# A graph layer's edge groups: one at a time, or in pairs

## The chip, the cores and the metric

The kernel runs on 1 core of a Trainium2 chip. The metric is the device time of one execution in microseconds (us); lower is better. The engines are PE (TensorE, the matrix engine; its weight loads are shown as PEld), DVE (VectorE), ACT (ScalarE), POOL (GpSimd) and SP (SyncE). SP, ACT and POOL also issue DMAs, each from its own queue. Every engine runs its own instruction stream in order and waits for others through semaphores.

## The reference, cut to what matters

N = 12,500 nodes with 64 features, E = 200,000 edges sorted by `dst`, all in float32.

```python
def ssp(x): return softplus(x) - log(2.0)
nodes    = x[[src, dst]]                                # (E, 128): both ends of each edge
gates    = ssp(edge_attr @ We1 + be1) @ We2 + be2       # (E, 64)
gates    = gates * (1 - sigmoid(5 * (dist - 3.5)))      # "cut" below
h        = ssp(nodes @ Wn1 + bn1) @ Wn2 + bn2           # (E, 64)
sums     = zeros(N, 64).at[dst].add(h * gates)          # the messages, added up per node
new      = x + ssp(sums @ Ws1 + bs1) @ Ws2 + bs2
out      = layernorm(x + new)
```

## The kernel before

The edges go in 391 groups of 512 (`NG` = 391). A group has two halves of 256 edges (h = 0, 1) and each half two blocks of 128 (t = 0, 1), so four blocks (k). As `dst` is sorted, the destinations of a half lie in a window of `W` = 42 consecutive nodes; `sums` stays in SBUF, with features on the partitions and nodes along the row (half 0 on partitions 0 to 63, half 1 on 64 to 127).

The code lies under a manual schedule: each engine's instructions stand in the order in which the Python code emits them, and a framework adds the semaphore waits from the tiles that an instruction reads and writes. Each of the tile names below has a number of buffers that are used in turn, and a new use waits for the last reader of the old one.

A prologue (to about 146 us) computes `table` = x @ Wn1 (the lower half) + bn1 for all nodes and writes it to DRAM, computes `cut`, and starts gathers. Then comes the loop over steps i = -1 to 388. In step i, each with the functions and profile lines that matter:

- `load` (L278, L286, on SP): one DMA of 256 KB of edge features for two groups (`eT`), and for each group two DMAs that put the window's 42 table rows below the constant rows of `wns`. They wait for an old scatter.
- `fetch` (L257, on SP and ACT): rows of x for a few blocks come by single-row DMAs, 7 a step on SP and 9 a step on ACT, between ACT's other instructions in threes.
- `gather` (L231, on POOL): the other blocks' rows of x by indirect DMA, 128 rows each, up to four a group; `xg` has 19 buffers (`AHEAD` 14 + `BEHIND` 5). POOL has no other work in the loop, so it runs ahead until a buffer is missing: the gathers of group g wait for the scatter of group g - 19, the last reader of that buffer.
- `transposes` (L307, L304, PE): the four blocks of group i+1, rows of x beside the one-hot of the destination in the window, become features by edges in PSUM (`tx`). `xcopy` (L314, ACT) copies that to SBUF (`xT`).
- `layer1_bias` (L319), `layer1_edge` (L324), `layer1_node` (L330), all PE: the first layer of group i+1 into `z` (two PSUM banks): 256 columns for the edges, where the two halves share the partitions, and 512 for the nodes, where the one-hot rows pick the destination's term from `wns`. The node matmuls wait for `xcopy`.
- `exps` (L341) and `logs` (L344) on ACT and `softplus` (L349) on DVE: softplus of the 768 columns into `s`.
- `layer2_bias` (L354), `layer2_edge` (L361), `layer2_node` (L366), PE: the second layer of group i, edge-major: blocks of `s` are the stationary operand, so its result `gh` has edges on the partitions: 2 matmuls of 128 columns and 4 of 64, which the profile shows as 4 and 8 records (a float32 matmul has two).
- `hcut` (L375) and `message` (L379) on DVE: h times `cut`, times the gates, 256 columns each.
- `scatter` (L383, PE): the messages of an older group times the one-hots, 84 columns, into a free part of `z`; `window` (L400, DVE) adds that to `sums`, two adds of 42 columns. `behind_by(i)` says which group: two behind, and from `CLOSE` = 12 steps before the end on one behind.
- `onehot` (L293, DVE) of group i+3; parts of `node_block` (the update and layernorm of up to 512 finished nodes, 25 blocks) at steps planned by `BLOCK_STEPS`.

So PE's order in a step is transposes i+1, biases, scatter, layer 1 edges i+1, layer 1 nodes i+1, layer 2 i. ACT's is copy, exp, log with three fetches behind each. DVE's is window sums, h, message, softplus, one-hot. POOL's is the gathers alone.

PSUM has eight banks: `z` two tiles of two banks, `gh` and `tx` two of one each.

Of the kernel before, what the change touches and what calls it, by code (L numbers as in the profile page):

```python
# [42 lines left out]
F32 = mybir.dt.float32  # L43
# [14 lines left out]
P = 128  # L58
# [10 lines left out]
SPREADS = 5  # L69
PREPARE = 5  # L70
BEHIND = 5
CLOSE = 12


BLOCK_STEPS = ((2, 3, 4, 4, 6, 7, 8, 9, 10, 14), (2, 3, 3, 4, 5, 6, 7, 8, 9, 10), (1, 2, 1, 2, 3))
# [48 lines left out]
def gnn_resnorm_kernel(ctx: ExitStack, tc: tile.TileContext, a: dict, out: bass.AP, E: int):  # L124
# [53 lines left out]
    one = const.tile([P, 1], F32, name="one")  # L178
    half = const.tile([P, 1], F32, name="half")
    eps = const.tile([P, 1], F32, name="eps")  # L180
    ones3 = const.tile([PIECES, HE], BF16, name="ones3")
    be3 = const.tile([PIECES, 2, D], BF16, name="be3")
    row3 = const.tile([PIECES, 2, K, D], BF16, name="row3")
    rs3 = const.tile([PIECES, K, D], BF16, name="rs3")
    wns = const.tile([DW, REST, 2, 2 * D], F32, name="wns")

    xgs, xrs, eTs = {}, {}, {}
    made = {}

    def note(key, ins):  # L190
# [80 lines left out]
    bases = {}  # L271

    def load(g):
        old = ("scatter", g - LOADS - 4)
        if g % 2 == 0:
            n = min(2, NG - g)
            both = loads.tile([P, 2, HE], F32, name="eT", bufs=4)
            behind(note(("load", g), nc.sync.dma_start(both[:, :n], a["eT"][:, g : g + n, :])), old)  # L278
            for j in range(n):
                eTs[g + j] = both[:, j]  # L280
            _, at = nc.values_load_multi_w_load_instructions(
                base_i[32:33, 2 * g : 2 * g + 4], engines=[SP], min_val=0, max_val=8 * D * (N - 1),
                skip_runtime_bounds_check_because="they were clamped to these bounds")
            bases[g], bases[g + 1] = at[:2], at[2:]
        for h in range(2):
            behind(note(("load", g), nc.sync.dma_start(  # L286
                wns[D:DW, g % REST, h, :].bitcast(U8),
                table_bytes[:, bass.ds(bases[g][h], 8 * D * W)].rearrange("o (w f) -> (o w) f", w=W))), old)
# [27 lines left out]

    def layer1_bias(g, *needs):
        zs[g] = z_tile()
        first = nc.tensor.matmul(zs[g][:, 0, :HE], be3.rearrange("q h d -> q (h d)"), ones3, start=True, stop=False,  # L319
                                 skip_group_check=True)  # L320
        behind(first, *needs)

# [14 lines left out]

    def exps(g, part=every):
        if part.start == 0:
            us[g] = work.tile([P, 3 * HE], F32, name="u")  # L340
        nc.scalar.activation(us[g][:, part], z_of(g)[:, part], AF.Exp)  # L341

    def logs(g, part=every):
# [1 line left out]

    def softplus(g, part=every):
        if part.start == 0:
            ss[g] = work.tile([P, 3, 2, P], F32, name="s", bufs=3)
        nc.vector.scalar_tensor_tensor(ss[g].rearrange("p i t e -> p (i t e)")[:, part], us[g][:, part], BIG,  # L349
                                       z_of(g)[:, part], OP.min, OP.max)  # L350

# [43 lines left out]
    def window(g):  # L395
        if g not in window_at:
            window_bases(g)
        for h in range(2):
            part = sums[h * D : (h + 1) * D, bass.ds(window_at[g][h], W)]
            nc.vector.tensor_add(part, part, scs[g][h * D : (h + 1) * D, h * W : (h + 1) * W])  # L400

    def node_block(first, n, pool):

# [86 lines left out]
    with tc.manual_schedule():  # L490
# [4 lines left out]
        with tc.tile_pool(name="prep", bufs=1) as prep:  # L495
# [81 lines left out]
                    nc.vector.tensor_sub(rest, rest, pieces[:, q, :])  # L577
            nc.scalar.dma_start(row_d.rearrange("(o q) f -> o q f", o=1), pieces)
            rows = prep.tile([PIECES, 4, D], BF16, name="rows")
            nc.scalar.dma_start(rows.rearrange("q i d -> q (i d)"), row_d)  # L580
            for i in range(3, PARTS):
                load_x(i)
# [3 lines left out]
            for i in range(PARTS):  # L586
                for c in range(i * CP, (i + 1) * CP, CP // 2):
                    m = CP // 2
                    ps = z_tile().rearrange("p b (k f) -> p (b k) f", k=K)
                    for k in range(m):  # L590
                        nc.tensor.matmul(ps[:, k, :], xT[:, c + k, :], wnb, start=True, stop=True)  # L591
                    tb = prep.tile([P, m, 2 * D], F32, name="tb", bufs=6)
                    nc.scalar.copy(tb[:, :K, :], ps[:, :K, :])
                    nc.vector.tensor_copy(tb[:, K:, :], ps[:, K:m, :])
                    nc.sync.dma_start(by_node[:, c : c + m], tb)
                    nc.vector.memset(sums[:, c * P : WIDE if c + m == NCH else (c + m) * P], 0.0)
                if i == 1:
                    nc.vector.tensor_copy(base_i[:1], base_b[:1])
                    nc.vector.tensor_scalar(base_i[32:33], base_b[32:33], float(8 * D), None, OP.mult)
                    nc.vector.tensor_scalar(rows_i, rows_i, float(4 * D), None, OP.mult)  # L600
                    for k in range(2):
                        nc.vector.tensor_copy(be3[:, k, :], rows[:, 0, :])
                    for k in range(K):
                        nc.vector.tensor_copy(row3[:, :, k, :], rows[:, 1:3, :])
                        nc.vector.tensor_copy(rs3[:, k, :], rows[:, 3, :])
                if i == 2:
                    nc.scalar.activation(dist, dist, AF.Sigmoid, bias=steep, scale=-5.0)
                    nc.scalar.preload_act_table_set("natural_log_exp_and_others")
                    nc.vector.tensor_copy(rel, dst_i)
                    for t in range(2):  # L610
                        r = rel[:, :, 2 * t : 2 * t + 2]
                        nc.vector.tensor_sub(r, r, base_b[:, :NH].rearrange("p (g h) -> p g h", h=2))


        with tc.tile_pool(name="finish", bufs=1) as finish:
            blocks = list(zip(node_blocks(N), block_steps(N, NG)))
            last = NG - 1
            parts, begun, complete, rest = {}, None, 0, []

            def at(f, g, *more):  # L620
                if 0 <= g < NG:
                    f(g, *more)

            def behind_by(i):
                close = last - CLOSE
                return [g for g in ([i - 2] if i <= close else []) + ([i - 1] if i >= close else []) if g >= 0]

            for g in range(LOADS - 1):
                load(g)
            for g in range(2):  # L630
                onehot(g)
            for i in range(-1, last - 1):
                now = parts.pop(i, [])
                early = [part for part in now if part.tensor]
                at(load, i + LOADS)
                read_rows(i, 0, ROWS[0])
                fetch(i, 0, ROWS[0])
                if i >= 0:
                    at(gather, i + AHEAD)
                transposes(i + 1, ("load", i + 1), ("gather", i + 1), ("onehot", i + 1))  # L640
                xcopy(i + 1)
                read_rows(i, 1, ROWS[1])
                fetch(i, 1, ROWS[1] - 6)
                layer1_bias(i + 1)
                at(layer2_bias, i)
                for n, g in enumerate(behind_by(i)):
                    scatter(g, zs[i + 1][:, 1, HE + 2 * n * W : HE + 2 * (n + 1) * W])
                layer1_edge(i + 1)
                layer1_node(i + 1)
                exps(i + 1)  # L650
                fetch(i, 1, 3)
                logs(i + 1)
                fetch(i, 1, 3)
                for g in behind_by(i):
                    window(g)
                at(layer2, i)
                for part in early:
                    part.tensor(tx_tile())
                at(hcut, i)
                at(message, i)  # L660
                softplus(i + 1)
                for part in early:
                    part.others()
                at(onehot, i + 3)
                for part in now:
                    if not part.tensor:
                        part.others()
                complete = i
                if blocks and complete >= blocks[0][1] - PREPARE and not begun:
                    begun = node_block(*blocks[0][0], finish)  # L670
                    begun.pop(0).others()
                if blocks and complete >= blocks[0][1]:
                    steps = next(steps for steps in BLOCK_STEPS if i + steps[-1] < last - 1)
                    for n, part in zip(steps, begun):
                        parts.setdefault(i + n, []).append(part)
                    rest = begun[len(steps) :]
                    blocks.pop(0)
                    begun = None
            assert len(blocks) == 1 and begun and not parts


# [43 lines left out]
    with tc.If(far > 0), tc.tile_pool(name="outside", bufs=1) as o:  # L725
# [7 lines left out]
        with tc.For_i(0, NG, 1) as g:  # L733
# [20 lines left out]
            for k in range(K):  # L754
# [1 line left out]
            xT = o.tile([P, NB], F32, name="xT2")  # L756
            nc.vector.tensor_copy(xT, z[:, 0, :])
            z = z_tile()
            nc.tensor.matmul(z[:, 1, :HE], be3.rearrange("q h d -> q (h d)"), ones3, start=True, stop=False,
                             skip_group_check=True)  # L760
            nc.tensor.matmul(z[:, 1, :HE], we1.rearrange("a h d -> a (h d)"), e, start=False, stop=True,
                             skip_group_check=True)
# [110 lines left out]
```

## Time and profile before

| | |
|---|---|
| median of 10 runs | 2680.15 us (2665.99 to 2698.31) |
| the profiled execution's own time | 2677.73 us |
| its span, first to last instruction | 2675.9 us |
| mean granted TensorE clock | 0.825 |
| busy: PE, PEld, DVE | 2216.0, 1731.5, 1050.9 us |
| busy: ACT, POOL | 968.4, 1437.0 us |
| gathers (L231) | 1516, mean 948 ns, idle before them 1138.8 us |
| first and last copy (L314) of the loop | start at 146.4 and 2652.2 us |

A line of a timeline reads: start in us, duration in us, engine, source line, operation, output<-inputs, shape, count, and in brackets how long the engine had been idle and what ended that. A line of a group reads: line, engine, operation, tiles, count, then busy us and mean ns of one, then the idle time before and its releasers. Ends of matmuls are modelled; releasers are inferred, and "remote" or "issue" stand where none was found. PEclk is the clock that the throttle granted, as a share of full speed.

### The profile page before, as it was taken

How to read it: one execution, taken by the hardware profiler on the slowest of the kernel's cores; microseconds unless marked ns; L12 is line 12 of the kernel's file. 1: busy time of each engine (PE TensorE's matmuls, PEld its weight loads, DVE VectorE, ACT ScalarE, POOL GpSimd, SP SyncE). 2: the span in 40 equal slices, each digit the busy share in tenths (PEclk: the TensorE clock that was granted, in tenths of full speed). 3: DMA queues.
4: the chain of work that ended last, by engine and by line, in shares of the span. 5: the costliest groups of instructions: out<-in, count | busy, mean ns of one | idle time of the engine just before them, and what ended most of it. 6: DMA issues, size and time to landing. Idle time of an engine off the chain costs nothing.

```text
span 2675.9 us, 47845 instructions
## 1 busy us (share of the span) xinstructions
PE 2216.0 (83%) x11373; PEld 1731.5 (65%) x11373; DVE 1050.9 (39%) x2767; ACT 968.4 (36%) x1318; POOL 1437.0 (54%) x1520
## 2 busy tenths in 40 slices
PE   2388889888888888888888888889889888888897
PEld 1366667666666666666666666666667666666676
DVE  1233333333334343343333444434434444444445
ACT  0133333333333333333333433333333433333344
POOL 7335555555555555555555555555555555555530
PEclk9987877878888788788887878888877988778788
DMA  6222212212222222222222222222222222222210
GB/s 159 75 69 53 49 47 47 48 46 52 48 50 50 49 52 50 49 47 52 51 47 51 50 54 52 51 51 56 53 48 52 53 57 54 51 51 51 50 49 21
DMA packets 150911, 143.53 MB, mean 54 GB/s; under 512 B 51887, under 2 KB 98395, under 8 KB 150626
## 3 DMA queue, kind: packets, MB, share of 16 engines
q1 hardware_dynamic: 94090, 88.26, 11.7%
q0 software_dynamic: 48512, 49.77, 9.5%
q10 hardware_dynamic: 8024, 2.37, 0.4%
q8 instruction: 97, 1.59, 0.2%
q14 instruction: 188, 1.54, 0.2%
HBM read 130.59 MB, written 9.63 MB: 52 GB/s over the span
## 4 chain that ended last, share of the span: by engine, by line
PE 61%; ACTq 11%; another core or an unknown queue 11%; ACT 7%; issue 6%; DVE 2%; POOL 1%; DMA 1%; DVEq 0%; SPq 0%; POOLq 0%
PE z L330 15%; PE gh L366 11%; ACTq L257 10%; PE z L383 10%; PE gh L361 7%; PE tx L307 6%; ACT xT L314 6%; PE z L324 3%; PE gh L354 3%; PE z L319 2%; PE tx L419 1%; PE z L591 1%; POOL xg L231 1%; ACTq L245 1%
## 5 line engine op out<-in xcount | busy, mean ns | idle before, releaser
L231 POOL DMA_INDIRECT xg<-in_x,src_i x1516 | 1436.7, 948 | 1138.8 <-issue 355.0
L330 PE MATMUL z<-xT,wns 106*128 106x256 f32 x1564 | 564.3, 496 | 340.8 <-ACT xT L314 330.2
L330 PEld LDWEIGHTS z<-xT,wns 106*128 106x128 f32 x1564 | 355.8, 242 | 503.7 <-ACT xT L314 431.4
L341 ACT ACTIVATE u<-z 128x768 f32<-128x768 f32 x392 | 317.0, 809 | 809.1 <-PE z L330 352.5
L366 PE MATMUL gh<-consts,s 128*128 128x64 f32 x3128 | 488.1, 311 | 0.0
L366 PEld LDWEIGHTS gh<-consts,s 128*128 128x128 f32 x3128 | 483.3, 236 | 0.1
L400 DVE TENSOR_TENSOR sums<-sums,z 64x42 f32 x778 | 153.0, 197 | 838.1 <-issue 621.8
L314 ACT COPY xT<-tx 106x512 f32<-106x512 f32 x391 | 228.6, 585 | 681.1 <-remote 260.5
L375 DVE TENSOR_TENSOR h<-gh,cut 128x256 f32<-128x256 f32 x391 | 166.0, 425 | 634.2 <-PE z L383 271.2
L344 ACT ACTIVATE u<-u,one 128x768 f32<-128x768 f32 x392 | 365.9, 933 | 70.2 <-issue 55.8
L349 DVE SCALAR_TENSOR_TENSOR s<-u,z 128x768 f32<-128x768 f32 x392 | 369.2, 942 | 10.9 <-ACT u L344 9.8
L361 PEld LDWEIGHTS gh<-consts,s 128*128 128x128 f32 x1564 | 295.6, 240 | 69.1 <-DVE s L349 32.6
L383 PEld LDWEIGHTS z<-xg,msg 128*128 128x128 f32 x1556 | 237.6, 219 | 151.0 <-issue 146.7
L361 PE MATMUL gh<-consts,s 128*128 128x128 f32 x1564 | 305.2, 328 | 1.8 <-DVE s L349 1.8
L383 PE MATMUL z<-xg,msg 128*128 128x84 f32 x1556 | 303.0, 324 | 0.9 <-DVE msg L379 0.2
L324 PE MATMUL z<-eT,consts 128*128 128x256 f32 x782 | 291.9, 460 | 0.0
L307 PE MATMUL tx<-consts,xg 128*106 128x128 f32 x1517 | 276.9, 311 | 6.4 <-DMA wns<-table 6.4
L307 PEld LDWEIGHTS tx<-consts,xg 128*106 128x106 f32 x1517 | 215.1, 168 | 10.4 <-issue 7.7
L379 DVE TENSOR_TENSOR msg<-gh,h 128x256 f32<-128x256 f32 x391 | 165.9, 424 | 13.4
L354 PE MATMUL gh<-row,ones 3*128 3x512 bf16 x391 | 168.4, 431 | 0.0
L324 PEld LDWEIGHTS z<-eT,consts 128*128 128x128 f32 x782 | 140.0, 224 | 1.2 <-issue 1.2
L293 DVE TENSOR_TENSOR xg<-consts,rel 128x168 f32<-128x168 f32 x391 | 129.1, 330 | 0.0
(93 smaller groups left out, 612.7 us busy)
## 6 DMA issues: line engine op xcount, KB each, us to landing
xr<-in_x ACTq DMA_DIRECT2D x3328, 0.2 KB
eT<-in_eT SPq DMA_DIRECT2D x195, 256.0 KB
xr<-in_x SPq DMA_DIRECT2D x2688, 0.2 KB
xg<-in_x,src_i POOLq DMA_INDIRECT x1516
wns<-table SPq DMA_DIRECT2D x782, 21.0 KB
table<-tb SPq DMA_DIRECT2D x14, 448.0 KB
sums<-in_xT SPq DMA_DIRECT2D x7, 455.0 KB
y<-in_x SPq DMA_DIRECT2D x24, 128.0 KB
```

What stands on the lines that cost most here:

```text
L231: note(("gather", g), nc.gpsimd.indirect_dma_start(out=xg[:, k, :D], out_offset=None, in_=x, in_offset=bass.IndirectOffsetOnAxis(ap=src_i[ ...
L257: ins = queues[queue].dma_start(row_tiles[n, "in"][r : r + 1, :D].bitcast(U8), x_bytes[:, bass.ds(row_at[queue].pop(0), 4 * D)])
L307: ins = nc.tensor.transpose(tx[:, k, :], xgs[g][:, k, :DW], ident)
L314: note(("xcopy", g), nc.scalar.copy(xT, xTs[g]))
L324: nc.tensor.matmul(zs[g][:, 0, :HE], we1.rearrange("a h d -> a (h d)"), eTs[g], start=False, stop=True, skip_group_check=True)
L330: nc.tensor.matmul(zn, wns[:, g % REST, h, :], xTs[g][:, h], start=True, stop=True, skip_group_check=True)
L341: nc.scalar.activation(us[g][:, part], z_of(g)[:, part], AF.Exp)
L344: nc.scalar.activation(us[g][:, part], us[g][:, part], AF.Ln, bias=one)
L349: nc.vector.scalar_tensor_tensor(ss[g].rearrange("p i t e -> p (i t e)")[:, part], us[g][:, part], BIG, z_of(g)[:, part], OP.min, OP.max)
L361: nc.tensor.matmul(v[:, 0, t], ss[g][:, 0, t, :], we2, start=False, stop=False, skip_group_check=True)
L366: nc.tensor.matmul(ghs[g][:, 1, 2 * t + h, :], ss[g][:, 1 + h, t, :], wn2, start=False, stop=h == 1 and t == 1, skip_group_check=True)
L383: ins = nc.tensor.matmul(sc, msgs[g][:, 2 * t : 2 * t + 2, :].rearrange("p h f -> p (h f)"), xgs[g][:, 2 * t : 2 * t + 2, D:DW], start=t = ...
```

## The change

Groups 0 to 379 go in 190 pairs (`PAIRS` = 190); group 380 is taken over by the single steps, which do the last 11 as before. For a pair p (groups 2p and 2p+1):

- Layer 1's edges of both groups are one matmul of 512 columns behind one bias matmul (`pair_edge`); the nodes stay two matmuls of 256 columns a group (`pair_node`). The first group's nodes share the two banks of `z1` with the edges of both; the second group's have a bank of `z2`, whose other bank takes scatters.
- exp, log and softplus take 1024 columns (edges of both, nodes of the first) and then 512 (nodes of the second).
- Layer 2 is feature-major: `we2` and `wn2` are the stationary operand and `s` streams, 512 columns: one matmul for the gates, two for h (one for each half, into the upper and the lower 64 partitions). ACT adds the gates' bias (`pair_bias`), DVE adds the other and multiplies (`pair_products`). Four PE transposes turn the products to edge-major (`pair_turn`, into the bank of h), and DVE multiplies by `cut` (`pair_weigh`).
- The scatters of both groups stand together, one pair behind, and so do their four window sums.
- Two rows of biases become a column each (`sides2`) in the prologue. `load` waits for an older scatter and is issued one group earlier; `onehot` one group earlier.

The pair's loop body, in PE's order: transposes A; bias and edges; gates (p); nodes A; transposes B; h (p); scatters (p-1); nodes B; turn (p). In ACT's: copy A, gates' bias (p), exp A, copy B, log A, exp B, log B, with the fetches between. In DVE's: weigh (p-1), one-hots, products (p), softplus A, window sums (p-1), softplus B.

```diff
-CLOSE = 12
+PAIRS = 190
...
-        old = ("scatter", g - LOADS - 4)
+        old = ("scatter", g - LOADS - 8)
...
+    def pair_edge(p):
+        z1s[p] = z_tile()
+        nc.tensor.matmul(z1s[p][:, 0], be3.rearrange("q h d -> q (h d)"), ones3, start=True, stop=False,
+                         skip_group_check=True)
+        nc.tensor.matmul(z1s[p][:, 0], we1.rearrange("a h d -> a (h d)"), eT2s[p], start=False, stop=True,
+                         skip_group_check=True)
...
+    def pair_exps(p, j):
+        u2s[p, j] = work.tile([P, (2 if j else 4) * HE], F32, name=f"u{j}", bufs=1)
+        nc.scalar.activation(u2s[p, j], pair_z(p, j), AF.Exp)
...
+    def pair_gates(p):
+        gates2[p] = gh_tile()
+        nc.tensor.matmul(gates2[p], we2.rearrange("a h d -> a (h d)"), s2s[p][:, :NB], start=True, stop=True,
+                         skip_group_check=True)
+
+    def pair_hidden(p):
+        hidden2[p] = gh_tile()
+        nodes = s2s[p][:, NB:].rearrange("p (j h e) -> p h j e", j=2, h=2)
+        for h in range(2):
+            nc.tensor.matmul(hidden2[p][h * D : (h + 1) * D].rearrange("p (j e) -> p j e", j=2), wn2, nodes[:, h],
+                             start=True, stop=True, skip_group_check=True)
+
+    def pair_bias(p):
+        turned2[p] = work.tile([P, NB], F32, name="mT")
+        nc.scalar.activation(turned2[p], gates2[p], AF.Identity, bias=sides2[:, 0:1])
+
+    def pair_products(p):
+        nc.vector.scalar_tensor_tensor(turned2[p], hidden2[p], sides2[:, 1:2], turned2[p], OP.add, OP.mult)
+
+    def pair_turn(p):
+        for t in range(K):
+            part = slice(t * P, (t + 1) * P)
+            nc.tensor.transpose(hidden2[p][:, part], turned2[p][:, part], ident)
+
+    def pair_weigh(p):
+        msg2s[p] = work.tile([P, 2, K, D], F32, name="msg2")
+        nc.vector.tensor_mul(msg2s[p].rearrange("p j k d -> p (j k) d"), hidden2[p].rearrange("p (k d) -> p k d", d=D),
+                             cut[:, 2 * p : 2 * p + 2, :].rearrange("p j k -> p (j k)").to_broadcast([P, 2 * K, D]))
+
+    def pair_scatter(p, sc):
+        for j in range(2):
+            msgs[2 * p + j] = msg2s[p][:, j]
+            scatter(2 * p + j, sc[:, j * 2 * W : (j + 1) * 2 * W])
...
+            for p in range(-1, PAIRS):
+                i, m, single = 2 * p, 2 * p + 2, p == PAIRS - 1
...
+                for j in range(2):
+                    at(load, i + LOADS + 1 + j)
+                for j in range(2):
+                    read_rows(i + j, 0, ROWS[0])
+                    fetch(i + j, 0, ROWS[0])
+                    if p >= 0:
+                        at(gather, i + AHEAD + j)
+                transposes(m, ("load", m), ("gather", m), ("onehot", m))
+                xcopy(m)
...
+                    pair_edge(p + 1)
+                if p >= 0:
+                    pair_gates(p)
+                    pair_bias(p)
+                if p >= 1:
+                    pair_weigh(p - 1)
...
+                    pair_node(p + 1, 0)
+                    pair_exps(p + 1, 0)
+                    transposes(m + 1, ("load", m + 1), ("gather", m + 1), ("onehot", m + 1))
+                    xcopy(m + 1)
...
+                    pair_logs(p + 1, 0)
...
+                if p >= 0:
+                    pair_hidden(p)
...
+                if p >= 0:
+                    pair_products(p)
...
+                    pair_scatter(p - 1, sc)
+                if not single:
+                    pair_node(p + 1, 1)
+                    pair_exps(p + 1, 1)
...
+                    pair_logs(p + 1, 1)
...
+                if p >= 0:
+                    pair_turn(p)
...
+                    pair_softplus(p + 1, 0)
...
+                if p >= 1:
+                    pair_windows(p - 1)
+                if not single:
+                    pair_softplus(p + 1, 1)
```

## The prediction

> **What bounds the kernel now.** I read the page first, then the timeline of single steps, the waits of the start, and busy time by stretches. The page names PE, with two oddities: a copy on ACT that waits for something "remote", and a clock that is not full.
>
> ```profile
> PE 2216.0 (83%) x11373; PEld 1731.5 (65%) x11373; DVE 1050.9 (39%) x2767; ACT 968.4 (36%) x1318; POOL 1437.0 (54%) x1520
> L231 POOL DMA_INDIRECT xg<-in_x,src_i x1516 | 1436.7, 948 | 1138.8 <-issue 355.0
> L314 ACT COPY xT<-tx 106x512 f32<-106x512 f32 x391 | 228.6, 585 | 681.1 <-remote 260.5
> ```
>
> The 391 copies of L314, one a group, start from 146.4 to 2652.2 us: 6.43 us a group, 12.85 us for two. The timeline of one step, at granted clock 1.0, shows what a step waits for:
>
> ```profile
> 1255.25 0.94 POOL L231 DMA_INDIRECT xg<-in_x,src_i  x1 [1.33 <-PE z L383]
> 1256.49 0.94 POOL L231 DMA_INDIRECT xg<-in_x,src_i  x1 [0.30 <-issue]
> 1257.20 1.00 PE L366 MATMUL gh<-consts,s 128*128 128x64 f32 x8
> 1257.74 0.95 POOL L231 DMA_INDIRECT xg<-in_x,src_i  x1 [0.30 <-issue]
> 1258.04 0.60 PE L307 MATMUL tx<-consts,xg 128*106 128x128 f32 x4
> 1258.99 0.94 POOL L231 DMA_INDIRECT xg<-in_x,src_i  x1 [0.30 <-issue]
> 1259.00 0.68 PE L383 MATMUL z<-xg,msg 128*128 128x84 f32 x4
> 1261.12 0.42 DVE L375 TENSOR_TENSOR h<-gh,cut 128x256 f32<-128x256 f32 x1 [2.88 <-PE z L383]
> 1261.20 0.58 ACT L314 COPY xT<-tx 106x512 f32<-106x512 f32 x1 [2.30 <-remote]
> 1261.51 0.94 POOL L231 DMA_INDIRECT xg<-in_x,src_i  x1 [1.58 <-remote]
> ```
>
> PE has done layer 2 (L366) at 1258.20, the transposes (L307) at 1258.64 and the scatter (L383) at 1259.68. Their three readers, h on DVE, the copy on ACT and the next gather on POOL, all start at 1261.1 to 1261.5. Nothing else stands in their waits. What ended just then is the last gather: 1258.99 + 2.2. The trace's semaphore events say the same for all steps: ACT's and DVE's updates appear 10 ns after their instruction, at every percentile up to the 99th; PE's are mostly on time up to 1.5 us after the first gather of a run and mostly held from 2.0 us on; between 2.5 and 4.25 us at most 3 in 100 are on time. They come 2.2 us after the start of the run's last gather. Outside runs all 167 were on time. Of 102 transposes that ended 3.0 to 3.5 us into a run of four, 101 copies started at 5.75 to 6.25 us. The first update in the held stretch sometimes slips out earlier (L366: a sixth to two fifths of those left, at each gather's end), those behind it do not.
>
> At the start, where 76 gathers run without a gap, the hold is longest. The third z tile is ready at 35.56, and ACT gets it at 88.04:
>
> ```profile
> 32.20 3.36 PE L591 MATMUL z<-consts,sums 65*128 65x128 f32 x14 [7.45 <-DVE tb L594]
> 88.04 0.58 ACT L593 COPY tb<-z 128x512 f32<-128x512 f32 x1 [38.62 <-remote]
> ```
>
> So the step is a loop: scatter's update, gathers (they take the buffers that the scatter frees), PE's held updates, the next scatter's update. With n gathers, 1.25 us apart, it lasts (n-1) x 1.25 + 2.2 + 0.3: for four 6.25 (1255.25 to 1261.51 is 6.26), for the mean of 3.88 (1516/391) 6.1. PE's gap inside it has a price. Columns: busy time of PE, PEld, DVE, ACT, POOL, then the clock:
>
> ```profile
> 1215.90:1223.90 8.00, 7.35 (x27) 6.02 (x28) 2.58 (x8) 2.92 (x4) 3.80 (x4) 0.50 0.11 22
> 1247.80:1261.20 13.40, 11.27 (x70) 7.77 (x69) 4.92 (x14) 5.47 (x7) 7.55 (x8) 1.00 0.23 50
> ```
>
> After a gap the clock is 0.50 for some 8 us and PE sets the step. That mix makes 6.43 of 6.1.
>
> **The change, part by part (for one pair).** PE, by the chain's pieces at full clock (half the 0.5-clock piece where only that is seen). Removed: two layer-1 biases 2 x 0.21, two layer-2 biases 2 x 0.22, two L324 2 x 0.46, L361 2 x 0.45, L366 2 x 0.84: 4.36. Added: one 512-column bias 0.22 (as L354), layer 1's edges and gates of 512 columns at 2 x 0.46 each, hidden with two matmuls of 512 at 1.84, four transposes 0.44: 4.34. PE's 8.1 us a pair stay. The two hidden matmuls write different halves of the partitions; no row here shows such a pair, so between 0.92 (overlapped) and 1.84; I take 1.84, as all matmuls in the trace follow each other.
>
> ACT: exp at 256, 512, 768 columns took 383, 577, 810 ns, Ln 507, 721, 935; by those steps 1024 cost 1.04 and 1.15, and a pair 3.49 before and after. The bias adds a 512-column pass, 0.58 (as L314). DVE: two softplus of 944 and four products of 425 (3.59) become 1.21 + 0.68 + 0.68 + 0.68 = 3.25. ACT's 18 and SP's 14 row fetches a pair, and the loads, stay in number; loads are issued a group earlier, so nothing waits for them. DVE gets one new wait: its window sums stand behind the exp of node B, and behind them its softplus and the product that frees hidden's bank; hidden would meet that only where node B is held (the 0.4 below covers it). Both engines are under 40% busy: the rest comes out at nothing, under the hold's cover; without it a pair of ACT's 5.2 or DVE's 4.7 is still under PE's 8.1.
>
> What matters is the order of releases. Gathers: 7.75 a pair. The two scatters of a pair are now one block, so both groups' buffers come free at once and POOL, which waits for nothing else, runs 7.75 gathers on end: 6.75 x 1.25 + 2.2 + 0.3 = 10.9 us from one release to the next, 1.3 us less than two runs (12.2). But PE's order has two round trips to ACT in a pair: transposes A, copy, node A; then transposes B, copy, node B. With one run a pair, one of them must fall outside it. Follow it. At a release the held scatter starts the next run at once. ACT does bias 0.58, exp 1.04 and only then copy B 0.59, with the sequencer's three fetches (0.9) between: 2.7 us. Node B ends at 3.6, inside the hold; so do the turn and transposes A (4.5). PE issues edges and gates, then waits for copy A until the next release, at 10.9. Now no scatter is pending and POOL stands still: copy A 0.59, node A 0.9 (four records 0.22 apart), transposes B 0.44, hidden 1.84, first scatter 0.54: 4.3 us at full clock (5.1 at the mean 0.825, up to 8.0 for the whole at 0.5) before the next run begins. This tail is the new wait. After such a free scatter copy B is ready, so node B, turn and transposes A follow at once; transposes A end some 2.1 us into the run, on the edge of the hold (L366 at 1.75 to 2.5 us: 5 of 23 on time; L330 in the same stretch: 125 of 127 by 2.5 us). If they pass, the next pair has no tail; if not, it has one.
>
> With p = 0.5, 1/(1+p) = 0.67 of the pairs pay the tail: 10.9 + 0.67 x 5.1 = 14.3. Where a held node B comes late, exp and Ln of 512 columns stand ahead of copy A on ACT (up to 2.0 us; 0.4 on average for a tail, as the front update often slips out): 14.55. Bounds: p = 1, full clock: 10.9 + 4.3/2 = 13.05; p = 0, half clock: 18.9.
>
> Sum: the profiled execution took 2677.7 (span 2675.9 and 1.8 around it; 2.4 under the median of 2680.15, the ten runs lie within 0.7% of that). Prologue, last 11 groups and node blocks stay. 190 x (14.55 - 12.85) = +323: **3000 us**.
>
> **Two rules of the Trainium skill.** The row is PE's held updates above. SBUF — State Buffer, section "SBUF: two separate sides", says that engine ports and DMA ports are apart and neither side can slow the other; by it there is no hold, the gathers' issue is the floor, and the sum is that of the second rival. I go by the rows, 101 of 102. The other row is the 0.50 after a gap. TensorE: Matmul & The Clock Gate, section "HAM oscillation", says that a gap over about 3.4 us puts PE back to half clock. It speaks against this change, whose wait for copy A can exceed that; with every tail at half clock the sum would be the third rival's.
>
> **Rivals.**
> *One release a pair (faster).* If transposes B or node B get out before the run ends, both trips share one release: 10.9 a pair, 2677.7 - 190 x 1.95 = 2310. It decides at a tail in under (12.85 - 10.9)/5.1 = 0.38 of the pairs. For it: front updates slip out. Against: the ones behind them don't, and two or three are pending. 0.18. With leaks in part, a tail in every second to third pair, 12.6 to 13.05 a pair, 2630 to 2716: 0.08 more, on both sides of no change.
> *No hold across a long run.* Then gathers bound it: 7.75 x 1.25 = 9.7 a pair, 2080. Against it stands the 38 us wait at the start. 0.06.
> *Half clock throughout.* Transposes A never pass, tail 8.0: 18.9 a pair, 3830; partly so, from 3350 up. For it: longer gaps than before. Against: eight busy microseconds bring the clock back. 0.10.
> *The change does not do what it says*: the changed kernel's instruction order has the 512-column matmuls and both groups' gathers behind one pair's scatters, so no chance.
>
> **Numbers.** The likeliest case has 0.58, its own range is 2720 (13.05 a pair) to 3350 (p = 0 at clock 0.825 and the 0.4: 16.4). Range 2300 to 3350: it leaves out the half clock (0.10), no hold (0.06) and a little of the single release (0.03). About 0.5% is what runs of this kernel can tell from no change. Faster by more than that: 0.18 + 0.06 + 0.02 = 0.26; within it 0.03; slower 0.58 + 0.10 + 0.03 = 0.71.
>
> **What would show it.** Right: L231 in runs of eight, 0.30 apart; copies that start 2.2 us after a run's last gather; pairs of about 11 and 16 us in turn; POOL idle some 4 to 5 us before a run; PEclk lower than 0.825. Wrong: pairs of 11 us throughout, copies that start inside a run, or POOL without gaps.

## The result, and the profile after

The changed kernel took 3057.46 us (median of 18 runs, 3045.93 to 3064.29) against 2679.20 us before (62 runs): a ratio of 1.1425, 95% interval 1.1404 to 1.1446. The profiled execution has a span of 3044.9 us. The forecast was 3000 us in a range of 2300 to 3350. The size of the sum held; the reason behind most of the loss did not.

From the page of the changed kernel, engines, chain, and the groups that answer to those shown of before:

```profile
PE 1987.9 (65%) x7765; PEld 1210.0 (40%) x7765; DVE 1007.4 (33%) x2390; ACT 1076.7 (35%) x1508; POOL 1439.8 (47%) x1520
...
SPq 13%; PE 12%; issue 9%; DMA 3%; ACTq 2%; ACT 1%; DVE 1%; another core or an unknown queue 0%; DVEq 0%
...
L232 POOL DMA_INDIRECT xg<-in_x,src_i x1516 | 1439.6, 950 | 1505.1 <-DVE mT L452 529.0
...
L309 PE MATMUL tx<-consts,xg 128*106 128x128 f32 x1517 | 291.0, 321 | 425.0 <-DMA wns<-table 329.5
...
L316 ACT COPY xT<-tx 106x512 f32<-106x512 f32 x391 | 227.1, 581 | 572.1 <-PE tx L309 211.8
...
L306 PE MATMUL tx<-consts,xr 128*106 128x128 f32 x47 | 18.0, 382 | 203.4 <-DMA xr<-in_x 203.4
```

PE and DVE got less to do, ACT 108 us more (1076.7 us, still only 35% of the span), and POOL's gathers cost what they did. Two things are new. SP's queue leads the chain with 13%; before, it had 0%. (The page follows the chain back only to 1762 us, so the shares add up to 42% of the span.) And PE's transposes, the first work of a group, wait for what SP's queue brings: 329.5 us (L309) for the table's rows in `wns`, 203.4 us (L306) for rows of x fetched one by one, 533 us together. (All 20 waits of L306 are for blocks that SP fetches, none for ACT's.) Before, the transposes had waited 6.4 us for `wns` and not at all for fetched rows. (L309 and L306 are the old L307 and L304; a pair's products on DVE, L452, start 14.82 us apart on average, median 13.21.)

The timeline of one pair shows both the old hold and the new wait:

```profile
1303.86 1.02 PE L385 MATMUL z<-xg,msg 128*128 128x84 f32 x8
1303.90 5.75 SPq L258 DMA_DIRECT2D xr<-in_x  x14
1304.70 0.94 POOL L232 DMA_INDIRECT xg<-in_x,src_i  x1 [2.67 <-PE z L385]
...
1313.21 3.71 SPq L288 DMA_DIRECT2D wns<-table  x4
1313.47 0.95 POOL L232 DMA_INDIRECT xg<-in_x,src_i  x1 [0.30 <-issue]
1315.58 1.07 PE L309 MATMUL tx<-consts,xg 128*106 128x128 f32 x4 [6.13 <-DMA wns<-table]
...
1316.68 0.59 ACT L316 COPY xT<-tx 106x512 f32<-106x512 f32 x1 [4.44 <-PE tx L309]
...
1323.83 1.12 PE L385 MATMUL z<-xg,msg 128*128 128x84 f32 x8
...
1324.78 0.95 POOL L232 DMA_INDIRECT xg<-in_x,src_i  x1 [10.36 <-DVE mT L452]
```

The pair's scatters (1303.86) free both groups' buffers, and eight gathers run on end, 1304.70 to 1313.47. PE then stands 6.13 us, but not for a held update: the four loads of `wns` are only being issued, from 1313.21 on. The next pair's gathers start 10.36 us after the end of the last.

Why SP is late shows in its own queue. In this view a row is a stretch of DMA issues: start, time from the first issue to the last, line, count. The gathers of the next two runs, seven and eight, start from 1324.78 to 1332.30 and from 1335.38 to 1344.12 (the view ends at 1345):

```profile
1317.86 5.37 SPq L258 DMA_DIRECT2D xr<-in_x  x14
1323.28 0.36 SPq L279 DMA_DIRECT2D eT<-in_eT  x1
1324.34 1.79 SPq L288 DMA_DIRECT2D wns<-table  x4
1327.10 10.76 SPq L258 DMA_DIRECT2D xr<-in_x  x14
1337.91 0.37 SPq L279 DMA_DIRECT2D eT<-in_eT  x1
1339.71 5.07 SPq L288 DMA_DIRECT2D wns<-table  x3
```

With no gathers in flight, 14 fetches take 5.37 us, and a whole round (1317.86 to 1327.10, its end in the first 2.3 us of the next run) 9.24. Under the first run and its release the same 14 take 10.76, and three loads under the second 5.07. Instruction by instruction, SP's records show the rate: in the first 3 us of a run about 4.5 a microsecond, between runs 4.8, and from 3 us after a run's first gather until 2.2 us after its last gather's start 1.3. There SP goes in steps of about 0.72 us. It has 43.7 instructions a pair: 32.8 of them follow the one before within 0.5 us (5.1 us in all), 8.1 within 0.5 to 1.0 us (5.8 us), 2.8 after more than that (3.9 us). These intervals add up to the pair, 14.8 us (15.0 in the expectations below), whatever bounds it. What tells is how little of them is waiting for a semaphore: over the whole run SP's loads (L279, L288) waited 39 us, less than 0.3 us a pair, where run 1 below has 1446 us. The largest entry for a load in each queue's list of waits (total us, times, longest), first of the changed kernel, then of run 1:

```profile
SPq L288 <- DMA wns<-table: 7.7, 9, 1.2
...
SPq L288 <- PE z L385: 519.2, 99, 8.3
```

SP has next to no time left, which makes its queue the suspected bound; the experiments test that.

The trace of before held the sign, in the same view of SP's queue:

```profile
1317.60 3.82 SPq L257 DMA_DIRECT2D xr<-in_x  x7
...
1323.28 2.55 SPq L257 DMA_DIRECT2D xr<-in_x  x7
```

Seven fetches, 2.55 us or 3.82. There SP spent some of its time waiting for scatters (82.6 and 34.0 us in its waits; all waits of its loads come to 133 us, some 0.7 us for two groups, so it had little to spare). In the kernel before, the slow stretches cover 5.3 us of a pair (runs of four), in the changed one 7.5 (runs of eight).

### The profile page after: what moved, and what is told of

Read it like the earlier page. It is cut to its first block, busy times and chain, and to the rows that moved or that the text cites. A ratio compares the mean times of both kernels' runs of the same rounds, so it can differ in the third digit from the quotient of the medians.

```text
span 3044.9 us, 40638 instructions
## 1 busy us (share of the span) xinstructions
PE 1987.9 (65%) x7765; PEld 1210.0 (40%) x7765; DVE 1007.4 (33%) x2390; ACT 1076.7 (35%) x1508; POOL 1439.8 (47%) x1520
## 5 line engine op out<-in xcount | busy, mean ns | idle before, releaser
L452 DVE SCALAR_TENSOR_TENSOR mT<-gh,sides,mT 128x512 f32<-128x512 f32 x190 | 142.6, 751 | 1428.1 <-PE gh L444 634.0
L309 PE MATMUL tx<-consts,xg 128*106 128x128 f32 x1517 | 291.0, 321 | 425.0 <-DMA wns<-table 329.5
L432 DVE SCALAR_TENSOR_TENSOR s<-u,z 128x1024 f32<-128x1024 f32 x380 | 362.9, 955 | 409.7 <-issue 279.5
L427 ACT ACTIVATE u<-u,one 128x1024 f32<-128x1024 f32 x380 | 355.5, 936 | 218.0 <-issue 150.6
L309 PEld LDWEIGHTS tx<-consts,xg 128*106 128x106 f32 x1517 | 212.8, 156 | 475.2 <-issue 451.5
L424 ACT ACTIVATE u<-z 128x1024 f32<-128x1024 f32 x380 | 308.1, 811 | 253.4 <-remote 77.9
L449 ACT ACTIVATE mT<-gh,sides 128x512 f32<-128x512 f32 x190 | 130.6, 687 | 715.8 <-PE gh L437 241.5
L410 PE MATMUL z<-eT,consts 128*128 128x512 f32 x380 | 321.8, 942 | 0.0
L437 PE MATMUL gh<-s,consts 128*128 128x512 f32 x380 | 276.3, 819 | 0.0
L444 PE MATMUL gh<-s,consts 128*64 128x512 f32 x760 | 215.0, 645 | 2.6 <-ACT mT L449 2.4
L306 PE MATMUL tx<-consts,xr 128*106 128x128 f32 x47 | 18.0, 382 | 203.4 <-DMA xr<-in_x 203.4
L457 PE MATMUL gh<-consts,mT 128*128 128x128 f32 x760 | 140.8, 317 | 0.0
L461 DVE TENSOR_TENSOR msg<-gh,cut 128x512 f32<-128x512 f32 x190 | 129.8, 683 | 0.0
```

The lines of the kernel that those rows point to most:

```text
L309: ins = nc.tensor.transpose(tx[:, k, :], xgs[g][:, k, :DW], ident)
L410: nc.tensor.matmul(z1s[p][:, 0], we1.rearrange("a h d -> a (h d)"), eT2s[p], start=False, stop=True, skip_group_check=True)
L424: nc.scalar.activation(u2s[p, j], pair_z(p, j), AF.Exp)
L427: nc.scalar.activation(u2s[p, j], u2s[p, j], AF.Ln, bias=one)
L432: nc.vector.scalar_tensor_tensor(s2s[p][:, slice(4 * HE, 6 * HE) if j else slice(0, 4 * HE)], u2s[p, j], BIG, pair_z(p, j), OP.min, OP.max)
L437: nc.tensor.matmul(gates2[p], we2.rearrange("a h d -> a (h d)"), s2s[p][:, :NB], start=True, stop=True, skip_group_check=True)
```

## The experiments

Theory T is the prediction's: a tail, the second round trip to ACT, falls behind the run of gathers. Theory S: SP's queue is the bound. The chips differ by up to 1.6% (the kernel before took 2642.71, 2639.67 and 2682.87 us in the three sets), so ratios to the kernel before on the same chip are compared.

| run | edit on | median us | ratio to before, 95% interval |
|---|---|---|---|
| the change itself | | 3057.46 | 1.1425 (1.1404 to 1.1446) |
| 1 no rows on SP | after | 2514.31 | 0.9531 (0.9463 to 0.9598) |
| 2 no rows on SP | before | 2582.34 | 0.9785 (0.9716 to 0.9854) |
| 3 both transposes first | after | 3029.50 | 1.1473 (1.1388 to 1.1559) |
| 4 edits 1 and 3 | after | 2529.04 | 0.9589 (0.9521 to 0.9656) |
| 5 split scatter | after | 2889.69 | 1.0963 (1.0903 to 1.1023) |
| 6 longer lead | after | 2996.44 | 1.1346 (1.1299 to 1.1394) |
| 7 no rows at all | after | 2607.42 | 0.9888 (0.9836 to 0.9939) |
| 8 no gathers | after | 2003.04 (one run) | |
| 9 five rows on SP | after | 2730.64 | 1.0188 (1.0125 to 1.0251) |
| 10 three rows on SP | after | 2585.35 | 0.9642 (0.9580 to 0.9704) |
| 11 edits 1 and 5 | after | 2674.23 | 0.9958 (0.9923 to 0.9993) |
| 12 edits 3 and 7 | after | 2583.00 | 0.9618 (0.9538 to 0.9697) |

### 1 and 2: no rows from SP's queue

```diff
-ROWS = (7, 9)
+ROWS = (0, 9)
```

> The changed kernel with no rows fetched from SP's queue: the 21 blocks of 128 rows that SP fetched row by row come by gathers instead (0.11 more gathers a pair, 1.25 us each: +0.14 us a pair, +26 in all). Theory T (the prediction's tail: PE's updates are held across a run of gathers, and one of two round trips to ACT falls behind it): SP's queue plays no part, so 3057 + 26, 3050 to 3100. Theory S (SP's queue is the bound: the trace of the changed kernel shows SP issuing a fetch in 0.32 us outside the runs, but one instruction per 0.72 us from some 4 us into a run until 2.2 us after its last gather, and hardly ever waiting; PE's transposes stood 329.5 us for the loads from the table and 203.4 for fetched rows): SP's 9.2 free us a pair lose 14 fetches of 0.32 and two register loads of 0.8, 6.1 us, so the step falls to what the tail leaves, under 13.1 us a pair: 2750 or less.

> The kernel before with the same edit: no rows fetched from SP's queue, their blocks by gathers. In its trace SP waits for scatters (82.6 and 34.0 us), so its queue has room, and both theories expect only the added gathers: 21 x 1.25 = 26 us, 2680 + 26 = 2705.

The changed kernel falls from 1.1425 to 0.9531, below the kernel before. This carries theory S, and it is more than the 307 us that S had asked for. The waits of PE for SP's queue are gone, and what paces a pair is again one run of gathers and the release behind it. The transposes on the page of run 1:

```profile
L309 PE MATMUL tx<-consts,xg 128*106 128x128 f32 x1538 | 279.4, 309 | 6.5 <-DMA wns<-table 6.5
```

Of 329.5 us 6.5 are left, and the row fetches (L306) have none. The timeline of one release in run 1, after a run whose last gather starts at 1304.69:

```profile
1304.69 0.94 POOL L232 DMA_INDIRECT xg<-in_x,src_i  x1 [0.30 <-issue]
...
1307.09 1.02 PE L385 MATMUL z<-xg,msg 128*128 128x84 f32 x8
1307.38 0.75 DVE L452 SCALAR_TENSOR_TENSOR mT<-gh,sides,mT 128x512 f32<-128x512 f32 x1 [3.26 <-PE tx L494]
1307.50 1.02 ACT L424 ACTIVATE u<-z 128x1024 f32<-128x1024 f32 x1 [2.28 <-PE tx L494]
...
1307.93 0.94 POOL L232 DMA_INDIRECT xg<-in_x,src_i  x1 [2.30 <-PE z L385]
```

DVE, ACT and POOL start within 0.6 us of one another, 2.7 to 3.2 us after the last gather's start. (DVE and ACT were held: their matmuls were done before 1306.2. POOL had to wait for the scatter itself, which PE began at 1307.09.) The products of pairs are 12.01 us apart in the mean; of 189 gaps 185 are under 13 us and none is over 16. There is one release a pair, and no tail, although PE's order is the one that the prediction followed.

The kernel before, with the same edit, was expected at +26 us and came out at 0.9785: the expectation missed, as SP's rows cost time there as well. PE's waits for SP do not account for it (6.4 us for `wns` before, 6.6 in run 2). What the trace shows is a sooner next run: behind a run of four its first gather starts a median of 2.33 us after the last start, 2.55 in the kernel before. Why SP's rows lengthen that is not shown, and a part of run 1's gain may be of this kind. With SP's queue out of the way in both kernels, the change on its own is a gain: 2514.31 against 2582.34, 2.6% less, measured on one chip.

### 3 and 4: the second round trip taken away

```diff
                 transposes(m, ("load", m), ("gather", m), ("onehot", m))
+                if not single:
+                    transposes(m + 1, ("load", m + 1), ("gather", m + 1), ("onehot", m + 1))
                 xcopy(m)
+                if not single:
+                    xcopy(m + 1)
...
-                    transposes(m + 1, ("load", m + 1), ("gather", m + 1), ("onehot", m + 1))
-                    xcopy(m + 1)
```

> The changed kernel with the transposes and the copy of the pair's second group moved up to stand right behind those of the first, so that a pair has one round trip to ACT ahead of its scatters and none of its own for group B. SP's queue is unchanged. Theory T: the tail is gone, one release a pair, 10.9 us a pair: 2310, up to 2500 with clock losses. Theory S: SP has the same work under the same runs, 14.8 us a pair: 2990 to 3070.

> Both edits on the changed kernel: both groups' transposes first, and no rows from SP's queue. Theory T: as the run with the transposes alone plus 26 us: 2340 to 2530. Theory S: neither queue nor tail is left, the run of 7.86 gathers sets the pair: (7.86-1) x 1.25 + 2.2 + 0.3 = 11.1 us, 2350 to 2550, and this well below the run with the transposes alone.

Run 3 is theory T's own test, and T falls as the reason of the loss: without the second round trip ahead of the scatters the ratio is 1.1473 instead of 1.1425. (A tail could still hide behind SP's queue there; run 1, where SP is no bound, has none.) Run 4 equals run 1 within the intervals (0.9589 and 0.9531), so the order of the transposes is worth nothing with SP's rows gone either.

### 5 and 11: two releases a pair

```diff
-    def pair_scatter(p, sc):
-        for j in range(2):
+    def pair_scatter(p, sc, only=range(2)):
+        for j in only:
...
-                    pair_scatter(p - 1, sc)
+                    pair_scatter(p - 1, sc, range(1))
...
                     pair_turn(p)
+                if p >= 1:
+                    pair_scatter(p - 1, sc, range(1, 2))
```

> The changed kernel with the scatter of a pair's second group moved behind the turn, so that the buffers of the two groups come free apart and the gathers go in runs of four instead of eight; SP's fetches stay. Theory S: SP's 44 instructions a pair took 15.0 us in the changed kernel (33 at full pace 5.1, 11 in slow steps 9.9); in the kernel before, with runs of four, they took 13.0 with waits. With runs of four the slow steps shrink to those of before: 12.7 to 13.2 us a pair, 2640 to 2750. If a pair's joint release is not what slows SP: 3000 to 3070.

> The changed kernel without SP's rows, with the second group's scatter moved behind the turn: two releases a pair. If releases set the pair there (PE's updates come 2.2 us after a run's last gather), two runs of 3.93 take 2 x (2.93 x 1.25 + 2.2 + 0.3) = 12.3 us against 12.0 with one: 2570. If PE's own work or ACT sets it: 2500 to 2530.

Run 5 missed: 2889.69 where 2640 to 2750 was expected. Its POOL trace says why: of its 243 runs (gathers whose starts lie less than 1.6 us apart) 94 have four gathers, but 104 eight and 24 seven. The slow stretches went from 7.5 to 7.0 us a pair, the pair from 14.82 to 14.02, and SP's loads still waited only 41 us in all. So the run agrees with S but does not undo the long runs. Run 11 shows what the split costs when SP is no bound: 12.84 us a pair against 12.01, more than the 12.3 expected, and a ratio of 0.9958 against 0.9531. Its runs merge as often (110 of four, 110 of eight, 15 of seven), so it is not SP's delay that merges them; what does is not shown, and neither run is a clean case of two releases a pair. Still, the joint scatter is a gain of the change, not its fault.

### 6: the loads a pair earlier

```diff
-AHEAD = 14
-LOADS = 5
+AHEAD = 12
+LOADS = 7
...
-            both = loads.tile([P, 2, HE], F32, name="eT", bufs=4)
+            both = loads.tile([P, 2, HE], F32, name="eT", bufs=5)
```

> The changed kernel with the loads of the table and of the edges issued one pair earlier (LOADS 5 to 7, one more edge buffer, and AHEAD 14 to 12 to make room for them); the order and the number of SP's instructions stay. Theory S, SP at its throughput: a longer lead adds no instruction rate, 3010 to 3080. Theory L, the loads only come late: PE's wait of 329.5 us for them goes, about 2750.

The ratio went from 1.1425 to 1.1346, far from 2750 us. The loads are on time now (PE's wait for them fell to 52.4 us), but the rows of a block are late instead: 366.8 us. The median pair takes 12.50 us, and 20 pairs, about one for each of SP's 21 blocks of rows, take 34 us in the mean. One of those waits on the timeline of run 6, with SP issuing without a break:

```profile
1466.50 5.78 SPq L258 DMA_DIRECT2D xr<-in_x  x14
...
1476.17 5.35 SPq L258 DMA_DIRECT2D xr<-in_x  x14
...
1482.21 0.46 PE L306 MATMUL tx<-consts,xr 128*106 128x128 f32 x1 [15.32 <-DMA xr<-in_x]
```

What is short is SP's rate, not the lead: lead only chooses which of its deliveries is the late one.

### 9 and 10: the dose

```diff
-ROWS = (7, 9)
+ROWS = (5, 9)
```

(and 3 for 5.)

> The changed kernel with 5 rows a group fetched from SP's queue instead of 7 (15 blocks instead of 21; the rest by gathers). Theory S, SP's rate: 4 fetches a pair less are 8 instructions of 0.155 and half a register load of 0.8, 1.6 us off 15.0: 13.4 a pair, 2745 (2690 to 2820). Rival, every fetched row costs the same share of the 543 us between the runs with 7 and with none: 2514 + 5/7 x 543 = 2902.

> The same with 3 rows a group. Theory S: SP needs 15.0 - 3.3 = 11.7 us a pair, less than the 12.0 that one run of gathers sets, so SP's queue is off the path: as with none, 2500 to 2560. Rival, every row costs the same share: 2514 + 3/7 x 543 = 2747.

With five rows a group, S had said 2745 us; it took 2730.64, and pairs are 13.10 us apart (13.4 expected), with 53 us of waits of SP's loads in all. The rival's 2902 is out (1.088 as a ratio, against 1.019). With three, 2585.35 is far nearer to S (2500 to 2560) than to the rival's 2747, though 25 us over. There SP's loads wait again, 541 us in all. So the cost is not one price a row: it grows from the point where SP's round is longer than the release of 12 us.

### 8: no gathers

```diff
-            if (g, k) in by_rows:
+            if (g, k) in by_rows or g >= AHEAD + BEHIND:
                 continue
```

> The changed kernel without the gathers of all groups past the first 19 (their node features stay those of earlier groups; all else is computed as before, rows on SP and ACT included). Theory S: with no runs there are no slow steps, and SP's own 44 instructions at full pace, 9.24 us a pair in the trace of the changed kernel, set the pair: 3057 - 190 x (14.8 - 9.3) = 2010, 1990 to 2080. If PE's work is the floor then (8.1 us a pair): about 1780.

One run, 2003.04 us; S had 2010 and PE's floor 1780. The pairs are 9.29 us apart. SP's queue, on its timeline, is back at full pace:

```profile
1304.25 5.38 SPq L258 DMA_DIRECT2D xr<-in_x  x14
1309.68 0.37 SPq L279 DMA_DIRECT2D eT<-in_eT  x1
1310.75 1.80 SPq L288 DMA_DIRECT2D wns<-table  x4
1312.65 5.33 SPq L258 DMA_DIRECT2D xr<-in_x  x14
```

No 14 fetches take 10.76 us any more. So the slow steps come with the gathers, and without them SP's 44 instructions are still about as long as the pair: SP's loads waited 66 us in all, and PE 104 us for what SP brings. ACT's queue stands high on this run's chain too (ACTq 27%, SPq 7%), so which of the two is the last limit at 9.3 us is not shown.

### 7 and 12: no rows on ACT either

```diff
-ROWS = (7, 9)
+ROWS = (0, 0)
```

> The changed kernel with no row fetches on SP or ACT: all blocks by gathers, 8 a pair. The run without SP's rows had 12.0 us a pair and ACT's fetches (L258) on 22% of its chain. Theory S extended to ACT's queue (ACT's issue also went in steps of 0.72 us from some 5.5 us into a run): the run of gathers sets the pair, 7 x 1.25 + 2.2 + 0.3 = 11.25 us, 2370 to 2470. If ACT's fetches are only on the chain because ACT waits anyway: the added 0.14 gathers a pair x 1.25 = +33 us on 2514, 2530 to 2560.

> The changed kernel without any row fetches and with both groups' transposes and copies first. In the run without rows 155 pairs took 8 to 14 us and 34 took 18 to 25. If those 34 are the prediction's tail (a second round trip to ACT that falls behind the run of gathers), one round trip a pair takes them away: about 11.5 us a pair, 2400 to 2450. If not: 2580 to 2630.

Run 7 missed both expectations: 0.9888, slower than with ACT's rows (0.9531). ACT's issue is slowed by long runs too (steps of 0.72 us, from 5.5 us into a run), but its fetches are no bound. Here 35 of the 189 pairs take over 16 us, 19.6 in the mean, and in one of them POOL stands 6.22 us before a run: that looks like the prediction's tail. With the second round trip away (run 12) 26 such pairs remain where the tail theory had none; the ratio is 0.9618. So round trips are at most part of it. Another part shows on POOL: in 18 of run 7's 35 long pairs the gathers of two pairs ran on end, 16 in a row, and in 10 of run 12's 26 they ran 12 or 16 in a row; run 1 has no run of more than eight. Why these pairs appear without ACT's fetches, and not with them, is open.

## Why the prediction was right in size and wrong in reason

**The hold on PE's updates: right.** In the prologue of the changed kernel, on its timeline, the third z tile is ready at 35.09 and ACT gets it at 88.30, as before:

```profile
31.73 3.36 PE L667 MATMUL z<-consts,sums 65*128 65x128 f32 x14 [7.96 <-issue]
...
88.30 0.59 ACT L669 COPY tb<-z 128x512 f32<-128x512 f32 x1 [38.61 <-remote]
```

**Runs of eight: right.** Of 186 runs in the loop 141 have eight gathers and 42 seven, mostly 0.30 us apart.

**One release in 10.9 us: mis-sized.** Run 1 shows the release alone: 12.0. With 7.86 gathers a pair, 6.86 x 1.25 = 8.6 us lie between the first and the last start of a run; the next run started a median of 3.2 us after the last (3.46 in the mean, and 8.6 + 3.46 makes the 12.0), not 2.2 + 0.3 as with runs of four. The hold is part of that: where two or more of PE's updates come out together, they do so a median of 2.66 us after the last start in run 1, 2.18 behind runs of four in the kernel before.

**The tail, 0.67 x 5.1 + 0.25 = 3.65 us a pair: wrong.** It was the step that turned a gain into a loss. Run 1, with PE's order unchanged, has none (0 of 189 pairs over 16 us), and run 3, which takes the second round trip away, gains nothing. The chance p that transposes A pass the hold was set at 0.5 from rows on the edge; where SP delivers in time the pairs run as if nearly all of them passed, or did not need to.

**"Loads are issued a group earlier, so nothing waits for them", and SP's fetches "at nothing, under the hold's cover": wrong.** This is the step that failed. The number of SP's instructions stays, as said, but not their length. The prediction asked whether the engines' busy time fits under the hold, and SP has no busy time in a profile. Its queue slows under the same runs that hold PE's updates, and the change made those runs longer. The price: 14.82 less 12.01 us a pair, 2.81 x 189 = 531 us, and PE's new waits for SP's deliveries are 329.5 + 203.4 = 533.

So 14.55 us was forecast as 10.9 + 3.65, and 14.82 came as 12.0 + 2.8. The sum fits by chance.

**PE's work: one term too large.** The two hidden matmuls, into different halves of the partitions, were taken one after the other at 1.84 us. On the timeline of the changed kernel, at full clock, they overlap:

```profile
1322.82 1.08 PE L444 MATMUL gh<-s,consts 128*64 128x512 f32 x4
```

That is near the bound of 0.92, so PE's pair is about 0.8 us lighter than 8.1. The Trainium skill, TensorEngine Tiling (Array Packing), section "Theoretical Speedup", allows up to twice the speed where a small dimension is at most 64; this row agrees, with 1.08 against 1.84. The prices on ACT and DVE held: exp 1.02, Ln 1.15, softplus 1.22, weigh 0.68; the bias took 0.69 for 0.58 and the products 0.75 for 0.68.

**The rivals.** "One release a pair" had the right mechanism for this change: it is what runs 1 and 4 show, at 12.0 us instead of 10.9. It was priced without SP's queue, which hides it. "No hold" and "half clock throughout" did not come; the mean clock fell from 0.825 to 0.789, while PE's busy share fell from 83% to 65%. Behind a gap of 6.13 us the edge matmul of a pair (L410, two records) took 2.08 us at a granted clock of 0.50, in run 1 without such a gap 1.13 us at 1.00. That agrees with the rule of the Trainium skill, TensorE: Matmul & The Clock Gate, section "HAM oscillation", that a gap over about 3.4 us puts PE back to half clock. It is a smaller part than the third rival made it.

**The rule of the Trainium skill, SBUF — State Buffer, section "SBUF: two separate sides"**, by which the sum would have been 2080, is out by some 980 us. The rule speaks of ports, and no run here shows whether a port is what holds PE's updates or slows SP. Run 8 comes to 2003 only by taking the gathers away.

**The signs named ahead.** Runs of eight, POOL idle before a run and a lower clock all came, yet not by the tail: they also fit a late SP. Pairs of 11 and 16 us in turn did not come; 87 of 189 were under 13 us and 47 over 16, with a mean of 21.0. That pattern alone spoke against the prediction's reason.

## What to carry to other kernels

An engine that only issues DMAs has a rate, and nothing on the page counts it as busy: count its instructions in one step of the loop, read their pace in the queue's timeline, beside and outside the other engine's bursts, and see how much of the step the queue spends waiting: next to nothing is the sign of a bound, to be tested by taking work off the queue. When a change makes a burst longer, ask of every queue what it manages under the burst. And when a forecast time is met, look at how it is spread over the steps before taking the reason as shown: a second, larger term can stand where the first was put.

## What the runs showed of the hardware that was not expected

- While indirect gathers run on POOL, SP's queue drops from 4.8 to 1.3 instructions a microsecond, in steps of about 0.72 us, from some 3 us after a run's first gather until 2.0 us (runs of four) to 2.6 us (runs of eight) after the start of its last; without gathers (run 8) the slow stretches are gone. ACT's row fetches show the same step, but only from about 5.5 us into a run. Why is not shown.
- The hold on PE's updates lasts longer after long runs: they come out a median of 2.66 us after the start of the last gather in run 1 (runs of seven to eight), 2.18 in runs of four in the kernel before. The next gather starts 3.2 and 2.55 us after that start.
- Taking all of ACT's 18 row fetches a pair away made the kernel slower (0.9531 to 0.9888), far beyond the 0.14 gathers a pair that took their place.

The best version measured is the change with no rows from SP's queue: 2514.31 us, 0.9531 (0.9463 to 0.9598) of the kernel before and below both kernels.
